# A bank of its own for the mixer's output products, three raw query products begun ahead, and another order in the routed layer's last tiles

## The chip, the cores and the metric

One core of a Trainium2 chip runs the whole network: a cross-attention layer, a state-space mixer and a routed low-rank layer, in float32. The metric is the device time of one execution in microseconds (us). Engines are named as in the profile: PE multiplies matrices (PEld is its weight load), DVE, ACT and POOL work element by element, SP starts the DMA transfers. Each engine takes its instructions in the order in which the program lists them; an instruction waits until the semaphores that it needs are reached, and what stands behind it on that engine waits too.

## The reference, cut to what matters

```python
x = x + xattn(layernorm(x), ctx, mask)   # x: 8 x 64 x 512, ctx: 8 x 1601 x 512
x = x + mixer(layernorm(x))
x = x + routed(layernorm(x))

# xattn: 32 query heads, 8 key heads of 128
q = rmsnorm(hidden @ q_proj_w.T) ; k = rmsnorm(ctx @ k_proj_w.T) ; v = ctx @ v_proj_w.T
out = softmax(q k^T / sqrt(128) + mask) v @ o_proj_w.T

# mixer: 64 heads of 64 channels in 8 groups, 128 states
gate, hbc, dt = split(h @ in_proj_w.T)
xs, B, C = silu(causal_conv4(hbc))
y = scan(state = state * exp(dt * A) + dt * xs * B ; y = state . C) + xs * D
y = y * rsqrt(mean of squares over the group) * norm_weight * silu(gate)
out = y @ out_proj_w.T

# routed: the best of 8 experts by logits = x @ route_w.T, each of rank 16
out = one_hot(argmax) * max(logits) * (x @ A.T) @ Bw
```

## The kernel before, in words

The 512 tokens are four tiles of 128. Nearly all projections are done by a scheme of seven block products in place of eight: a product of 2 x 2 blocks is put together from sums of weight blocks (S1 to S4, made by POOL in `weight_sums`, lines 142 to 150, in the order S1, S2, S3, S4 of which each but S3 needs one before it) and sums of input blocks (T1 to T4, made by DVE). `FIRST` (line 38) lists the products a, d, b, c; a takes raw blocks alone (L11, R11), d takes S2 and T2, b takes S1 and T1, c takes S3 and T3. `SECOND` (line 39) adds three further products into the banks of a, b and c: one of raw blocks, one with S4, one with T4.

**Query stage** (`project_queries`, lines 153 to 305). Sixteen pairs of heads go through `load` (line 172: 512 KB of weights wq_p by SP, then POOL's four sums), `first` (line 215: FIRST on PE, then the ACT copy q_p and the DVE sums q_u, q_t, q_raw), and `second` (line 234), which closes a pair after the next one's `first`. Weight buffers are three deep, and the PSUM banks ab and cd three each, so a pair's load is issued two pairs ahead. `load(0)` and `load(1)` stand in front, then the rest of the constants, 22 warm-up products, the layernorm and transposes of the four tiles (`layernorm_T`, line 124), and T1 to T4 (line 203). After every second pair `factors` (line 243) sums the squares of four heads (qss), makes their inverse root on ACT (qrs), and sends it through memory to be spread over all partitions (qrsb, 1 MB); `finish` (line 259) multiplies (q_st on DVE) and stores the four heads (q_d, 1 MB). The first keys' and values' weights wk and wv (512 KB each, `Loads.weights`, line 894), and the first context tiles (cx) are issued behind the load of pair 10 (`loaded[HQ // 2 - 6]`); their POOL sums stand where that order puts them, and each sum tile is stored at once for later batches.

**Attention** (`attend_all`) then runs over 8 batches x 4 pairs of key heads; the change touches there only where the first two of those stores are issued.

**Mixer** (`mixer_and_routed`, from line 968). For each of the eight groups g, PE makes six input projections (`project`, with the causal convolution on DVE, L1165, and a silu on ACT), while the steps of the group before (mix, scan, gate) stand between them. After the last silu ACT loads the table of exp and ln (line 121), and `decay` makes seg on PE (L1140) and dec on ACT (L1145) for the four tiles of the next group. Then come the gates of the group (`project_gates`, first and second, twice), and among them the four output products of the group before (`project_out`, line 1309: four products mo into one bank, and one DVE instruction, L1316, that adds them to x with the scale rs of `norm`, line 1295, whose sum pss PE makes just before). The order is written by hand with `issue_after`: first(0), mo 0, second(0), mo 1, first(1), mo 2, second(1), mo 3; decay and norm are bound to the table load only, so a planner puts them between. The eight PSUM banks are: pj three deep (projections, gates and mo), seg two (seg, pss and others), px, y0 and y1 one each; px holds the transposes of `layernorm_T` at the mixer's two ends. The last group has no projections behind it, so its own mix and scan stand between its gates (`own`).

**Routed layer** (`route`, line 1334), per tile, after the last group's four mo: layernorm and transposes, ph (PE), the choice of the best expert on DVE (top, rw, first, rw, wh), wt (a transpose on PE), whT (ACT), ro (PE), o = x + ro (DVE), and a store of 256 KB. Each tile's steps stand behind the next tile's mo.

Of the kernel before, what the change touches and what calls it, by code (L numbers as in the profile page):

```python
# [15 lines left out]
P = 128  # L16
# [107 lines left out]
def layernorm_T(nc, c, small, psum, x, tt, dst, tag="tr", bufs=1, pbufs=2, copy=None):  # L124

    st = small.tile([P, 6], F32, tag="ln_st", name="ln_st")
    nc.vector.bn_stats(st, x[:, tt, :])
    mv = small.tile([P, 2], F32, tag="ln_mv", name="ln_mv")
    nc.vector.bn_aggr(mv, st)
    rs = small.tile([P, 1], F32, tag="ln_rs", name="ln_rs")  # L130
    rsqrt_of_mean(nc, rs, mv[:, 1:2], 1.0, c.eps)
    xn = small.tile([P, D], F32, tag="ln_xn", name="ln_xn", bufs=bufs)
    nc.vector.tensor_scalar(
        xn, x[:, tt, :], mv[:, 0:1], rs, op0=ALU.subtract, op1=ALU.mult
    )
    tp = psum.tile([P, DC, P], F32, tag=tag, name="ln_tp", bufs=pbufs)
    for dc in range(DC):
        nc.tensor.transpose(tp[:, dc, :], xn[:, dc * P : (dc + 1) * P], c.ident)
    (copy or nc.vector.tensor_copy)(dst, tp)


def weight_sums(nc, l, out):

    s1, s2, s3, s4 = (out[:, k] for k in range(4))
    add = nc.gpsimd.tensor_tensor
    add(s1, l["L21"], l["L22"], ALU.add)
    add(s2, s1, l["L11"], ALU.subtract)
    add(s3, l["L11"], l["L21"], ALU.subtract)
    add(s4, l["L12"], s2, ALU.subtract)
    return dict(L11=l["L11"], L12=l["L12"], L22=l["L22"], S1=s1, S2=s2, S3=s3, S4=s4)  # L150


@with_exitstack
def project_queries(ctx, tc, c, x, wq, qw, q_d, rs_d):
# [25 lines left out]
        }  # L180
        weights.append(weight_sums(nc, l, wst.tile([P, 4, 2, HD], F32, tag="ws", name=f"wqs_{p}")))

    load(0)
    load(1)
    c.load_rest()
    xnT = big.tile([P, DC, NT], F32, name="xnT")

    warm = ps.tile([P, P], F32, tag="ss", name="warm", bufs=2)
    for _ in range(22):
        nc.tensor.matmul(warm, lhsT=c.ones, rhs=c.ones, start=True, stop=True)  # L190
    for tt in range(NTT):
        layernorm_T(
            nc, c, small, ps, x, tt, xnT[:, :, tt * P : (tt + 1) * P], tag="ss", bufs=2, pbufs=2,
            copy=nc.scalar.copy,
        )
    r = {
        f"R{e + 1}{half + 1}": xnT[:, 2 * e : 2 * e + 2, half * HT : (half + 1) * HT]
# [10 lines left out]
    def product(ps, lhs, rhs, start, stop):  # L208
        for dc in range(2):
            nc.tensor.matmul(  # L210
                ps, lhsT=lhs[:, dc, :], rhs=rhs[:, dc, :], start=start and dc == 0, stop=dc == 1,
                skip_group_check=True,
            )

    def first(p, quad):
        st = Pair()
        st.w, st.q, st.k = weights[p], quad.q, 2 * (p % 2)
        st.ps = {}
        for pair in ("ab", "cd"):
            t = ps.tile([P, 2, HT], F32, tag=pair, name=f"pq_{pair}_{p}", bufs=3)  # L220
            st.ps[pair[0]], st.ps[pair[1]] = t[:, 0, :], t[:, 1, :]

        for k, lhs, rhs in FIRST:
            product(st.ps[k], st.w[lhs], r[rhs], k in "ad", False)
        p1 = wk2.tile([P, HT], F32, tag="p1", name="q_p1")
        nc.scalar.copy(p1, st.ps["a"])
        st.u2 = wk2.tile([P, HT], F32, tag="u2", name="q_u2", bufs=3)
        nc.vector.tensor_tensor(st.u2, p1, st.ps["d"], ALU.add)
        t = wk2.tile([P, HT], F32, tag="t", name="q_t", bufs=1)
        nc.vector.tensor_tensor(t, st.u2, st.ps["b"], ALU.add)  # L230
        nc.vector.tensor_tensor(st.q[:, st.k + 1, HT:], t, st.ps["c"], ALU.add)
        return st
# [41 lines left out]
        )  # L274


    quads, open_ = [], []

    def close():
        st, quad = open_.pop(0)  # L280
# [2 lines left out]
        return quad if len(quad.sq) == 2 else None  # L283

    for p in range(HQ // 2):
        if p % 2 == 0:
            quad = Pair()
            quad.n, quad.sq = p // 2, []
            quad.q = late.tile([P, QD4, NT], F32, tag="q", name="q_raw", bufs=3)
            quads.append(quad)  # L290
        if p + 2 < HQ // 2:
            load(p + 2)
        open_.append((first(p, quad), quad))
        if p:
            done = close()
        if p % 2 == 1 and p > 1:

            factors(quads[p // 2 - 1])
            if p > 3:
                finish(quads[p // 2 - 2])  # L300
# [1 line left out]
    factors(quads[-1])  # L302
    finish(quads[-2])
    finish(quads[-1])
    return loaded[HQ // 2 - 6].ins


@with_exitstack
def attend_all(
# [399 lines left out]
    with tc.issue_after(queries_loaded):  # L709
        first.wk = loads.weights("wk", first)  # L710
        first.wv = loads.weights("wv", first)
        first.cx.load[0]()
        first.cx.load[1]()
        load_mask()
        load_q(first)
    for add in first.cx.sums[0]:
        add()
    def last_projection():
# [99 lines left out]
class Loads:  # L818
# [1 line left out]

    def __init__(self, nc, ctxp, wpool, ctxT, wk, wv, s_d):
        self.nc, self.ctxp, self.wpool, self.ctxT, self.s_d = nc, ctxp, wpool, ctxT, s_d
        self.w = dict(wk=wk, wv=wv)

    def context(self, b):

# [65 lines left out]
    def weights(self, name, u):  # L894

        nc, pr = self.nc, u.pr
        bufs = 1 if name == "wk" else 2
        raw = self.wpool.tile([P, DC, 2 * HD], F32, tag=name, name=f"{name}_{pr}", bufs=bufs)
        nc.sync.dma_start(
            out=raw,  # L900
            in_=self.w[name][:, pr * 2 * HD : (pr + 1) * 2 * HD].rearrange("(dc p) o -> p dc o", p=P),
        )
        l = {
            f"L{hh + 1}{e + 1}": raw[:, 2 * e : 2 * e + 2, hh * HD : (hh + 1) * HD]
            for hh in range(2) for e in range(2)
        }
        sums = self.wpool.tile([P, 4, 2, HD], F32, tag=f"{name}s", name=f"{name}s_{pr}", bufs=bufs)
        s1, s2, s3, s4 = (sums[:, k] for k in range(4))
        if u.b == 0:
            weight_sums(nc, l, sums)  # L910
            nc.sync.dma_start(out=self.s_d[name, pr], in_=sums)
        else:
            nc.sync.dma_start(out=sums, in_=self.s_d[name, pr])
        return dict(raw=raw, L11=l["L11"], L12=l["L12"], L22=l["L22"], S1=s1, S2=s2, S3=s3, S4=s4)
# [3 lines left out]
def cross_attention(ctx, tc, c, x, ctxT, lastT, maskT, wq, wk, wv, wo):  # L918
# [3 lines left out]
    big = ctx.enter_context(tc.tile_pool(name="xa_big", bufs=1))  # L922
    dram = ctx.enter_context(tc.tile_pool(name="xa_dram", bufs=1, space=bass.MemoryType.DRAM))
    qw = big.tile([P, 1], F32, name="qw")

    nc.vector.tensor_scalar(
        qw, c.qnw, c.knw, 1.0 / math.sqrt(HD), op0=ALU.mult, op1=ALU.mult
    )
    mask_sb = big.tile([P, NKT, S], F32, name="mask_sb")

    last_keys = big.tile([P, DC, B], F32, name="last_keys")
# [16 lines left out]
        rows_d.append(r)  # L948

    with tc.tile_pool(name="xa_ctx", bufs=1) as ctxp, tc.tile_pool(name="xa_w", bufs=1) as wpool:  # L950
        loads = Loads(nc, ctxp, wpool, ctxT, wk, wv, s_d)
        queries_loaded = project_queries(tc, c, x, wq, qw, q_d, rs_d)
        full = NKT - 1

        def load_mask():
            nc.sync.dma_start(
                out=mask_sb[:, :full, :], in_=maskT[: full * P, :].rearrange("(t p) q -> p t q", p=P)
            )
            nc.sync.dma_start(out=mask_sb[: KV - full * P, full, :], in_=maskT[full * P :, :])
            nc.sync.dma_start(out=last_keys, in_=lastT.rearrange("(dc p) b -> p dc b", p=P))  # L960

        return attend_all(
            tc, c, x, loads, mask_sb, load_mask, last_keys, q_d, o_d, v1_d, rows_d, wo, queries_loaded
        )
# [3 lines left out]
def mixer_and_routed(ctx, tc, c, x, done, w_in, w_out, w_ra, b_w, out):  # L968
# [337 lines left out]
            G.rs[tt] = rs[:, i : i + 1]  # L1306
        return last.ins

    def project_out(G, tt):
        po = bank("pj", [P, D], "mo", 3)  # L1310
        for n in range(GC):
            last = nc.tensor.matmul(  # L1312
                po, lhsT=G.y[:, n, tt * P : (tt + 1) * P], rhs=G.wo[:, n, :],
                start=n == 0, stop=n == GC - 1,
            )
        nc.vector.scalar_tensor_tensor(  # L1316
            out=x[:, tt, :], in0=po, scalar=G.rs[tt], in1=x[:, tt, :], op0=ALU.mult, op1=ALU.add
        )
        return last.ins
# [10 lines left out]
    def load_routed():  # L1330
        nc.sync.dma_start(out=w, in_=w_ra.rearrange("(dc p) o -> p dc o", p=P))
        nc.sync.dma_start(out=bw, in_=b_w)

    def route(tt):
        xnT = grpp.tile([P, DC, P], F32, tag="sq", name="rt_xnT")
        layernorm_T(nc, c, small, ps, x, tt, xnT, tag="px", bufs=2, pbufs=1, copy=nc.scalar.copy)
        ph = bank("seg", [P, E + E * R], "ph", 2)
        for dc in range(DC):
            nc.tensor.matmul(
# [20 lines left out]
        whT = wk.tile([P, P], F32, tag="whT", name="whT")  # L1360
        nc.scalar.copy(whT, pt)
        po = bank("y1", [P, D], "ro")
        nc.tensor.matmul(po, lhsT=whT, rhs=bw, start=True, stop=True)
        o = wk.tile([P, D], F32, tag="acc", name="o", bufs=3)
        nc.vector.tensor_tensor(o, x[:, tt, :], po, ALU.add)
        nc.sync.dma_start(out=out[tt * P : (tt + 1) * P, :], in_=o)


    g0 = groups[0]
# [97 lines left out]
    with tc.issue_after(table):  # L1467
        norm(G, range(NTT))
        for tt in range(NTT):
            project_out(G, tt)  # L1470
            if tt:
                route(tt - 1)
        route(NTT - 1)


@with_exitstack
# [63 lines left out]
```

## Time and profile before

| what | us |
|---|---|
| time, median of 3 runs | 2778.91 (2778.89 to 2780.34) |
| profiled execution | 2779.38 |
| its span | 2777.7 |
| PE busy in the span | 2739.1 (99%) |
| DVE, POOL, ACT busy | 1748.5, 809.3, 777.4 |
| query stage, first product to first key product | 11.43 to 130.01 |
| attention | 130 to about 2285 |
| mixer and routed layer | about 2285 to 2777.7 |

The mean granted clock of PE is 0.998 of full speed. In the rows that follow, a line of a timeline gives the start, the duration, the engine, the source line, the operation with its output and inputs, and in brackets how long the engine had been idle before and what ended the idle time. A line of the waits gives the waiting instruction, what released it, the total, the number of times and the longest. [...]

### The profile page before, as it was taken

How to read it: one execution, taken by the hardware profiler on the slowest of the kernel's cores; microseconds unless marked ns; L12 is line 12 of the kernel's file. 1: busy time of each engine (PE TensorE's matmuls, PEld its weight loads, DVE VectorE, ACT ScalarE, POOL GpSimd, SP SyncE). 2: the span in 40 equal slices, each digit the busy share in tenths (PEclk: the TensorE clock that was granted, in tenths of full speed). 3: DMA queues.
4: the chain of work that ended last, by engine and by line, in shares of the span. 5: the costliest groups of instructions: out<-in, count | busy, mean ns of one | idle time of the engine just before them, and what ended most of it. 6: DMA issues, size and time to landing. Idle time of an engine off the chain costs nothing.

```text
span 2777.7 us, 39019 instructions
## 1 busy us (share of the span) xinstructions
PE 2739.1 (99%) x14988; PEld 2006.3 (72%) x14988; DVE 1748.5 (63%) x3160; ACT 777.4 (28%) x1410; POOL 809.3 (29%) x818
## 2 busy tenths in 40 slices
PE   9999999999999999999999999999999998999998
PEld 7677777777778777778777777777787544555555
DVE  4556676566666666766666676667666316655666
ACT  3322223222222222223222222322222003333333
POOL 4323323322222233223322222232223113333321
PEclk9999999999999999999999999999999999999999
DMA  4821322231123213221312232122212452333421
GB/s 160 280 87 47 88 68 54 54 104 43 50 54 90 55 39 93 69 56 47 104 47 53 54 89 56 39 82 80 55 41 56 142 194 69 92 106 84 137 58 35
DMA packets 349571, 222.85 MB, mean 80 GB/s; under 512 B 223916, under 2 KB 308778, under 8 KB 348362
## 3 DMA queue, kind: packets, MB, share of 16 engines
q1 hardware_dynamic: 349386, 220.36, 28.2%
q8 instruction: 119, 1.95, 0.3%
q14 instruction: 66, 0.54, 0.1%
HBM read 189.26 MB, written 31.05 MB: 79 GB/s over the span
## 4 chain that ended last, share of the span: by engine, by line
PE 92%; DVE 4%; DMA 2%; issue 1%; ACT 1%; POOL 0%; SPq 0%; DVEq 0%; ACTq 0%; POOLq 0%
PE pav L602 13%; PE psc L532 12%; PE pv_a L451 6%; PE pv_b L451 6%; PE pv_c L451 6%; PE pk_b L391 6%; PE pk_c L391 6%; PE pk_a L391 6%; PE pj L1152 4%; PE mo L1312 4%; PE pv_d L451 3%; PE pk_d L391 3%; PE pj_ab L1210 2%; PE psn L420 2%; PE pq_ab L210 1%; PE pj_cd L1210 1%
## 5 line engine op out<-in xcount | busy, mean ns | idle before, releaser
L537 DVE SCALAR_TENSOR_TENSOR attn<-psc,rk,mask_sb 128x256 f32<-128x256 f32 (+1 forms) x832 | 364.4, 476 | 200.1 <-PE psc L532 192.4
L586 POOL TENSOR_TENSOR sm<-attn 128x512 f32<-128x512 f32 x64 | 81.8, 1279 | 1203.3 <-ACT attn L584 1203.3
L602 PE MATMUL pav<-attn,v 128*128 128x256 f32 (+1 forms) x1664 | 380.3, 379 | 0.0
L532 PE MATMUL psc<-q,kT 128*128 128x256 f32 x1536 | 367.1, 380 | 0.0
L589 POOL TENSOR_TENSOR sm<-sm,attn 128x512 f32<-128x512 f32 x256 | 339.4, 1326 | 29.5 <-DVE attn L580 10.7
L532 PEld LDWEIGHTS psc<-q,kT 128*128 128x128 f32 x1536 | 287.6, 190 | 76.3 <-issue 28.6
L602 PEld LDWEIGHTS pav<-attn,v 128*128 128x128 f32 (+1 forms) x1664 | 311.5, 190 | 42.3 <-issue 1.0
L580 DVE TENSOR_TENSOR attn<-attn,nb 128x1024 f32<-128x1024 f32 x192 | 224.9, 1215 | 49.7 <-ACT nb L577 49.6
L584 ACT ACTIVATE attn<-attn 128x1024 f32<-128x1024 f32 x192 | 203.1, 1058 | 80.7 <-DVE attn L580 77.7
L451 PEld LDWEIGHTS pv_a<-wv,cx 128*128 128x128 f32 x1536 | 193.9, 191 | 28.9 <-issue 22.1
L548 DVE TENSOR_TENSOR mx<-mx,attn 128x512 f32<-128x512 f32 x256 | 210.8, 823 | 2.0
L451 PE MATMUL pv_a<-wv,cx 128*128 128x128 f32 x1536 | 206.8, 277 | 0.0
L391 PE MATMUL pk_a<-cx,wk 128*128 128x417 f32 (+1 forms) x512 | 193.3, 500 | 0.8 <-ACT qrs L115 0.8
L1152 PE MATMUL pj<-mx_xnT,w_in 128*128 128x512 f32 x384 | 177.0, 602 | 0.0
L402 ACT ACTIVATE ksq<-kT 128x834 f32<-128x834 f32 (+1 forms) x128 | 109.3, 872 | 144.6 <-DVE kT L383 144.6
L391 PEld LDWEIGHTS pk_a<-cx,wk 128*128 128x128 f32 x512 | 97.2, 190 | 46.1 <-issue 20.8
L1312 PE MATMUL mo<-w_out,y 128*128 128x512 f32 x256 | 116.9, 597 | 10.5 <-issue 7.8
L1152 PEld LDWEIGHTS pj<-mx_xnT,w_in 128*128 128x128 f32 x384 | 68.8, 190 | 71.0 <-issue 68.7
L577 ACT COPY nb<-nbs 128x256 f32<-128x256 f32 x64 | 24.1, 376 | 301.8 <-DMA nbs<-max_d 285.3
L381 ACT COPY kT<-pk_a 128x384 f32<-128x384 f32 x64 | 31.6, 493 | 267.4 <-PE pk_a L391 267.4
L1165 DVE SCALAR_TENSOR_TENSOR acc<-pj,small_consts,acc 128x504 f32<-128x504 f32 (+1 forms) x144 | 103.9, 724 | 1.1
L649 POOL TENSOR_TENSOR o<-o,f 128x512 f32<-128x512 f32 x31 | 39.4, 1271 | 219.9 <-DMA f<-sums_d 182.2
(244 smaller groups left out, 4423.6 us busy)
## 6 DMA issues: line engine op xcount, KB each, us to landing
wk<-in_wk SPq DMA_DIRECT2D x32, 512.0 KB
wv<-in_wv SPq DMA_DIRECT2D x32, 512.0 KB
w_in<-in_w_in SPq DMA_DIRECT2D x16, 1024.0 KB
wvs<-wv_s_d SPq DMA_DIRECT2D x28, 512.0 KB
wks<-wk_s_d SPq DMA_DIRECT2D x28, 512.0 KB
cx<-in_ctxT SPq DMA_DIRECT2D x16, 834.0 KB
cx<-in_ctxT SPq DMA_DIRECT2D x16, 768.0 KB
wq<-in_wq SPq DMA_DIRECT2D x16, 512.0 KB
```

The source lines that it names most:

```text
L391: nc.tensor.matmul(ps[:, :w], lhsT=u.wk[l][:, dc, :], rhs=u.cx.r[ch][r][:, dc, :], start=start and dc == 0, stop=dc == 1, skip_group_check ...
L402: nc.scalar.activation(sq[ch][:, :, half, :w], u.kT[:, :, half, lo:hi], AF.Square)
L451: nc.tensor.matmul(ps[:, i * HD : (i + 1) * HD], lhsT=u.cx.r[ch][r][:, dc, i * P : (i + 1) * P], rhs=u.wv[l][:, dc, :], start=start and i ...
L532: nc.tensor.matmul(ps[:rows, t - t2, :], lhsT=lhsT, rhs=qh, start=True, stop=True)
L537: nc.vector.scalar_tensor_tensor(out=s.at[:rows, t, :].rearrange("p (h q) -> p h q", h=GQ), in0=ps[:rows, t - t2, :].rearrange("p (h q) -> ...
L548: nc.vector.tensor_tensor(s.mx2, s.mx2, s.at[:, t2 : t2 + 2, :], ALU.max)
L580: nc.vector.tensor_tensor(at[:, k : k + 4, :], at[:, k : k + 4, :], nb.unsqueeze(1).to_broadcast([P, 4, 256]), ALU.add,)
L584: nc.scalar.activation(at[:, k : k + 4, :], at[:, k : k + 4, :], AF.Exp)
L589: nc.gpsimd.tensor_tensor(sm2, sm2, at[:, i : i + 2, :], ALU.add)
L602: nc.tensor.matmul(s.av[:, 0, :], lhsT=u.v[:rows, t, hh, :], rhs=s.at[:rows, t, :], start=t == 0, stop=t == NKT - 1,)
L1152: done = nc.tensor.matmul(pj, lhsT=G.w[:, dc, n, :], rhs=xnT[:, dc, :], start=dc == 0, stop=dc == DC - 1).ins
L1312: last = nc.tensor.matmul(po, lhsT=G.y[:, n, tt * P : (tt + 1) * P], rhs=G.wo[:, n, :], start=n == 0, stop=n == GC - 1,)
```

## The change

- The first product (a) of a pair is split off into `begin`. Pairs 0, 1 and 2 are begun before `first` of pair 0; from pair 3 on a pair is begun just before its `first`. `first` takes b, d, c in place of d, b, c. Three loads stand in front in place of two. The DVE instruction for qw, which stood ahead of the first normalisation, goes behind the last, and the normalisations of tiles 2 and 3 are bound behind those of tiles 0 and 1. 16 warm-up products are left of 22.
- The first wk, wv and context loads are bound to the load of pair 11 in place of pair 10, and POOL's sums for wk and wv (of the first batch) to the last sum of the last query pair. The two stores of those first sums are issued after the first query load of the attention.
- In the program's order of SP the loads of wk and wv now stand behind wq_11 and wq_12, and wq_14 between the two halves of the first context load.
- `project_out` takes the bank px, one deep, in place of pj; the four calls after the last group keep pj.
- In `route`, two small products (`fill`) of ones follow the transposes for tiles 2 and 3 each; the last tile's ro, o and store are made in two halves; and the last tile's steps get the priority that tile 2's had. On PE all of ph of tile 3 then stands before wt and ro of tile 2, and on DVE the steps from top to wh of tile 3 before o of tile 2.

```diff
...
@@ -146,8 +147,8 @@
     add(s1, l["L21"], l["L22"], ALU.add)
     add(s2, s1, l["L11"], ALU.subtract)
     add(s3, l["L11"], l["L21"], ALU.subtract)
-    add(s4, l["L12"], s2, ALU.subtract)
-    return dict(L11=l["L11"], L12=l["L12"], L22=l["L22"], S1=s1, S2=s2, S3=s3, S4=s4)
+    last = add(s4, l["L12"], s2, ALU.subtract).ins
+    return dict(last=last, L11=l["L11"], L12=l["L12"], L22=l["L22"], S1=s1, S2=s2, S3=s3, S4=s4)
 
 
 @with_exitstack
@@ -180,18 +181,29 @@
         }
         weights.append(weight_sums(nc, l, wst.tile([P, 4, 2, HD], F32, tag="ws", name=f"wqs_{p}")))
 
-    load(0)
-    load(1)
-    c.load_rest()
+
+    AHEAD = 3
+    for p in range(AHEAD):
+        load(p)
+        if p == 1:
+            c.load_rest()
     xnT = big.tile([P, DC, NT], F32, name="xnT")
 
     warm = ps.tile([P, P], F32, tag="ss", name="warm", bufs=2)
-    for _ in range(22):
+    for _ in range(16):
         nc.tensor.matmul(warm, lhsT=c.ones, rhs=c.ones, start=True, stop=True)
+    norms = []
     for tt in range(NTT):
-        layernorm_T(
-            nc, c, small, ps, x, tt, xnT[:, :, tt * P : (tt + 1) * P], tag="ss", bufs=2, pbufs=2,
-            copy=nc.scalar.copy,
+
+        with tc.issue_after(norms[tt - 2]) if tt > 1 else nullcontext():
+            norms.append(layernorm_T(
+                nc, c, small, ps, x, tt, xnT[:, :, tt * P : (tt + 1) * P], tag="ss", bufs=2, pbufs=2,
+                copy=nc.scalar.copy,
+            ))
+
+    with tc.issue_after(norms[-1]):
+        nc.vector.tensor_scalar(
+            qw, c.qnw, c.knw, 1.0 / math.sqrt(HD), op0=ALU.mult, op1=ALU.mult
         )
     r = {
         f"R{e + 1}{half + 1}": xnT[:, 2 * e : 2 * e + 2, half * HT : (half + 1) * HT]
@@ -212,16 +224,21 @@
                 skip_group_check=True,
             )
 
-    def first(p, quad):
+    def begin(p, quad):
         st = Pair()
         st.w, st.q, st.k = weights[p], quad.q, 2 * (p % 2)
         st.ps = {}
         for pair in ("ab", "cd"):
             t = ps.tile([P, 2, HT], F32, tag=pair, name=f"pq_{pair}_{p}", bufs=3)
             st.ps[pair[0]], st.ps[pair[1]] = t[:, 0, :], t[:, 1, :]
-
-        for k, lhs, rhs in FIRST:
-            product(st.ps[k], st.w[lhs], r[rhs], k in "ad", False)
+        k, lhs, rhs = FIRST[0]
+        product(st.ps[k], st.w[lhs], r[rhs], True, False)
+        return st
+
+    def first(st):
+
+        for k, lhs, rhs in (FIRST[2], FIRST[1], FIRST[3]):
+            product(st.ps[k], st.w[lhs], r[rhs], k == "d", False)
         p1 = wk2.tile([P, HT], F32, tag="p1", name="q_p1")
         nc.scalar.copy(p1, st.ps["a"])
         st.u2 = wk2.tile([P, HT], F32, tag="u2", name="q_u2", bufs=3)
...
@@ -283,14 +300,18 @@
         return quad if len(quad.sq) == 2 else None
 
     for p in range(HQ // 2):
-        if p % 2 == 0:
-            quad = Pair()
-            quad.n, quad.sq = p // 2, []
-            quad.q = late.tile([P, QD4, NT], F32, tag="q", name="q_raw", bufs=3)
-            quads.append(quad)
-        if p + 2 < HQ // 2:
+        for i in range(AHEAD) if p == 0 else range(p, p + 1) if p >= AHEAD else ():
+            if i % 2 == 0:
+                quad = Pair()
+                quad.n, quad.sq = i // 2, []
+                quad.q = late.tile([P, QD4, NT], F32, tag="q", name="q_raw", bufs=3)
+                quads.append(quad)
+            begun.append((begin(i, quads[i // 2]), quads[i // 2]))
+        if AHEAD <= p + 2 < HQ // 2:
             load(p + 2)
-        open_.append((first(p, quad), quad))
+        st, quad = begun.pop(0)
+        first(st)
+        open_.append((st, quad))
         if p:
             done = close()
         if p % 2 == 1 and p > 1:
@@ -302,7 +323,7 @@
     factors(quads[-1])
     finish(quads[-2])
     finish(quads[-1])
-    return loaded[HQ // 2 - 6].ins
+    return loaded[HQ // 2 - 5].ins, weights[-1]["last"]
 
 
 @with_exitstack
@@ -713,6 +734,7 @@
         first.cx.load[1]()
         load_mask()
         load_q(first)
+        loads.store_sums()
     for add in first.cx.sums[0]:
         add()
     def last_projection():
@@ -820,9 +842,16 @@
 
 
 
-    def __init__(self, nc, ctxp, wpool, ctxT, wk, wv, s_d):
-        self.nc, self.ctxp, self.wpool, self.ctxT, self.s_d = nc, ctxp, wpool, ctxT, s_d
+    def __init__(self, tc, nc, ctxp, wpool, ctxT, wk, wv, s_d):
+        self.tc, self.nc, self.ctxp, self.wpool, self.ctxT, self.s_d = tc, nc, ctxp, wpool, ctxT, s_d
         self.w = dict(wk=wk, wv=wv)
+
+        self.stores = []
+
+    def store_sums(self):
+        for out, sums in self.stores:
+            self.nc.sync.dma_start(out=out, in_=sums)
+        self.stores = None
 
     def context(self, b):
 
@@ -907,8 +936,12 @@
         sums = self.wpool.tile([P, 4, 2, HD], F32, tag=f"{name}s", name=f"{name}s_{pr}", bufs=bufs)
         s1, s2, s3, s4 = (sums[:, k] for k in range(4))
         if u.b == 0:
-            weight_sums(nc, l, sums)
-            nc.sync.dma_start(out=self.s_d[name, pr], in_=sums)
+            with self.tc.issue_after(self.sums_behind):
+                weight_sums(nc, l, sums)
+            if self.stores is None:
+                nc.sync.dma_start(out=self.s_d[name, pr], in_=sums)
+            else:
+                self.stores.append((self.s_d[name, pr], sums))
         else:
             nc.sync.dma_start(out=sums, in_=self.s_d[name, pr])
         return dict(raw=raw, L11=l["L11"], L12=l["L12"], L22=l["L22"], S1=s1, S2=s2, S3=s3, S4=s4)
@@ -922,10 +955,6 @@
     big = ctx.enter_context(tc.tile_pool(name="xa_big", bufs=1))
     dram = ctx.enter_context(tc.tile_pool(name="xa_dram", bufs=1, space=bass.MemoryType.DRAM))
     qw = big.tile([P, 1], F32, name="qw")
-
-    nc.vector.tensor_scalar(
-        qw, c.qnw, c.knw, 1.0 / math.sqrt(HD), op0=ALU.mult, op1=ALU.mult
-    )
     mask_sb = big.tile([P, NKT, S], F32, name="mask_sb")
 
     last_keys = big.tile([P, DC, B], F32, name="last_keys")
...
@@ -1306,8 +1335,8 @@
             G.rs[tt] = rs[:, i : i + 1]
         return last.ins
 
-    def project_out(G, tt):
-        po = bank("pj", [P, D], "mo", 3)
+    def project_out(G, tt, tag="px"):
+        po = bank(tag, [P, D], "mo", 3 if tag == "pj" else 1)
         for n in range(GC):
             last = nc.tensor.matmul(
                 po, lhsT=G.y[:, n, tt * P : (tt + 1) * P], rhs=G.wo[:, n, :],
@@ -1331,9 +1360,17 @@
         nc.sync.dma_start(out=w, in_=w_ra.rearrange("(dc p) o -> p dc o", p=P))
         nc.sync.dma_start(out=bw, in_=b_w)
 
+    def fill(n):
+
+        t = bank("pj", [P, P], "fill", 3)
+        for _ in range(n):
+            nc.tensor.matmul(t, lhsT=c.ones, rhs=c.ones, start=True, stop=True)
+
     def route(tt):
         xnT = grpp.tile([P, DC, P], F32, tag="sq", name="rt_xnT")
         layernorm_T(nc, c, small, ps, x, tt, xnT, tag="px", bufs=2, pbufs=1, copy=nc.scalar.copy)
+        if tt >= NTT - 2:
+            fill(2)
         ph = bank("seg", [P, E + E * R], "ph", 2)
         for dc in range(DC):
             nc.tensor.matmul(
@@ -1360,10 +1397,14 @@
         whT = wk.tile([P, P], F32, tag="whT", name="whT")
         nc.scalar.copy(whT, pt)
         po = bank("y1", [P, D], "ro")
-        nc.tensor.matmul(po, lhsT=whT, rhs=bw, start=True, stop=True)
         o = wk.tile([P, D], F32, tag="acc", name="o", bufs=3)
-        nc.vector.tensor_tensor(o, x[:, tt, :], po, ALU.add)
-        nc.sync.dma_start(out=out[tt * P : (tt + 1) * P, :], in_=o)
+
+        n = 2 if tt == NTT - 1 else 1
+        for k in range(n):
+            cols = slice(k * D // n, (k + 1) * D // n)
+            nc.tensor.matmul(po[:, cols], lhsT=whT, rhs=bw[:, cols], start=True, stop=True)
+            nc.vector.tensor_tensor(o[:, cols], x[:, tt, cols], po[:, cols], ALU.add)
+            nc.sync.dma_start(out=out[tt * P : (tt + 1) * P, cols], in_=o[:, cols])
 
 
     g0 = groups[0]
@@ -1467,10 +1508,13 @@
     with tc.issue_after(table):
         norm(G, range(NTT))
         for tt in range(NTT):
-            project_out(G, tt)
+            project_out(G, tt, "pj")
             if tt:
+                ahead = tc.tile_snap_priority()
                 route(tt - 1)
-        route(NTT - 1)
+
+        with tc.high_priority(offset=tc.tile_snap_priority() - ahead):
+            route(NTT - 1)
 
 
 @with_exitstack
```

More of the change, by code (lines that the diff above doesn't have):

```diff
@@ L132, in layernorm_T @@
     xn = small.tile([P, D], F32, tag="ln_xn", name="ln_xn", bufs=bufs)
-    nc.vector.tensor_scalar(
+    norm = nc.vector.tensor_scalar(
         xn, x[:, tt, :], mv[:, 0:1], rs, op0=ALU.subtract, op1=ALU.mult
@@ L139, in layernorm_T @@
     (copy or nc.vector.tensor_copy)(dst, tp)
+    return norm.ins
 def weight_sums(nc, l, out):
@@ L274, in finish @@
         )
-    quads, open_ = [], []
+    quads, begun, open_ = [], [], []
     def close():
@@ L924, in cross_attention @@
     qw = big.tile([P, 1], F32, name="qw")
-    nc.vector.tensor_scalar(
-        qw, c.qnw, c.knw, 1.0 / math.sqrt(HD), op0=ALU.mult, op1=ALU.mult
-    )
     mask_sb = big.tile([P, NKT, S], F32, name="mask_sb")
@@ L950, in cross_attention @@
     with tc.tile_pool(name="xa_ctx", bufs=1) as ctxp, tc.tile_pool(name="xa_w", bufs=1) as wpool:
-        loads = Loads(nc, ctxp, wpool, ctxT, wk, wv, s_d)
-        queries_loaded = project_queries(tc, c, x, wq, qw, q_d, rs_d)
+        loads = Loads(tc, nc, ctxp, wpool, ctxT, wk, wv, s_d)
+        queries_loaded, loads.sums_behind = project_queries(tc, c, x, wq, qw, q_d, rs_d)
         full = NKT - 1
```

## The prediction

> **What bounds the kernel now.** I read the page first, then the waits of TensorE (PE), the timeline around each wait, the granted clock there, and the chain of the last 37 us.
>
> ```profile
> PE 2739.1 (99%) x14988; PEld 2006.3 (72%) x14988; DVE 1748.5 (63%) x3160; ACT 777.4 (28%) x1410; POOL 809.3 (29%) x818
> ```
>
> PE is busy for 2739.1 of 2777.7 us. No product is removed by the change, so all that it can win is among the 38.6 us without PE work, plus stretches where PE runs at a lower clock. The waits of PE (total us, times, longest) say where the 38.6 lie; these five bear on the change:
>
> ```profile
> PE mo L1312 <- issue: 7.8, 5, 1.7
> PE pq_cd L210 <- POOL wqs L147: 4.7, 3, 2.3
> ...
> PE mo L1312 <- DVE acc L1165: 2.6, 2, 1.8
> ...
> PE wt L1359 <- DVE wh L1352: 1.7, 1, 1.7
> ...
> PE pq_ab L210 <- DMA wq<-in_wq: 0.5, 1, 0.5
> ```
>
> The attention stage (130 to 2285 us) has only some 2.4 us of waits: it is PE throughout, so what the query stage wins is carried through it. The profiled execution took 2779.38 us, 0.47 above the median of 2778.91; I sum on the first and take 0.5 off.
>
> **Query stage.** The timeline at pair 11 of the weights, and the clock (columns: stretch, its length, PE busy, PE clock, DMA share, GB/s):
>
> ```profile
> 83.53 1.03 PE L210 MATMUL pq_ab<-xnT,wq 128*128 128x256 f32 x4
> 86.81 1.74 PE L210 MATMUL pq_cd<-xs,wqs 128*128 128x256 f32 x4 [2.25 <-POOL wqs L147]
> 88.34 1.91 PE L210 MATMUL pq_ab<-xs,wqs 128*128 128x256 f32 x4
> ```
>
> ```profile
> 84.00:88.00 4.00, 1.75 (x7) 0.90 0.83 256
> 88.00:92.00 4.00, 4.00 (x14) 0.67 0.79 268
> ```
>
> A product normally takes 0.86 us from start to start; the two after the wait took 1.5 and 1.7. The clock rows give half clock for 0.10 x 4 / 0.5 = 0.8 us and 0.33 x 4 / 0.5 = 2.6 us, together 3.4.
>
> 1. Pair 11: POOL made eight sums for wk and wv (0.72 us each, 78.95 to 84.7) before this pair's own. The change puts them behind the last query sums: -2.25, and with the wait its half clock goes: four products from 86.81 to 91.19 became 4.4 us instead of about 2.6, -1.75.
> 2. Pair 10 waited 1.38 us (78.25) for sums that began at 75.20, when wq_10 had landed; it was issued at 68.83 with wk and wv (1 MB) right behind it. In the new order wk is issued after wq_11 and wv after wq_12: -1.38. Also b is now taken ahead of d, and needs the first sum only: 0.86 us of cover.
> 3. Pair 14 waited 0.50 (DMA) and 1.11 (POOL). wq_14 took 9.8 us to land behind 768 KB of context, 1 MB of factors and 1 MB of query stores. In the new queue half the context stands behind it, and PE meets it with one and a half products more in hand: -1.61.
> 4. Front: PE now does a of three pairs before it needs sums. It waits for wq_1 and wq_2 (about 10.3 and 12.6), and two transposes queue behind that, so the DVE sums of x start some 0.4 later; at the first d (15.74 before, about 16.15 after) 1.5 products more are done, 1.29 us: -0.9. The shorter warm-up (16 for 22) ends in PE time that waits for the layernorm anyway; so does the moved qw (0.20 us of DVE), whose cover was none: it stood ahead of the first xn.
> 5. New waits. PE would come to pair 14 about 6 us sooner, but everything it needs must too: wq_14 stands behind the factor load of quad 4 in SP's queue, and on DVE four products q_st of quad 4 (waiting for that load) and two context sums of 0.95 us stand ahead of the u and t of pair 14, on which b of its second half waits. DMA moved 12.74 MB from 64 to 112 us, 265 GB/s; without the two sum stores (1 MB, now after the query loads) and in 42 us it would be 278 GB/s, against 350 to 390 in its fullest slices. From 0 to 4.7 us (1.5 queue, 1.7 DVE, 1.5 DMA): half, +2.4.
>
> Sum: -0.9 - 1.38 - 2.25 - 1.75 - 1.61 + 2.4 = -5.5 (from -3.2 to -7.9). The stores of wk and wv sums move later by 20 us or more of slack; nothing.
>
> **Mixer, boundaries of groups 1 to 6.** The timeline of one (all six have the same distances within 0.05 us; group 1 waits only 0.89):
>
> ```profile
> 2489.44 0.71 DVE L1165 SCALAR_TENSOR_TENSOR acc<-pj,small_consts,acc 128x488 f32<-128x488 f32 x1
> ...
> 2490.25 3.67 PE L1312 MATMUL mo<-w_out,y 128*128 128x512 f32 x8 [1.71 <-issue]
> ...
> 2492.76 0.64 ACT L1145 ACTIVATE dec<-seg 128x256 f32<-128x256 f32 x2
> 2493.86 0.66 PE L1140 MATMUL seg<-av,past 64*64 64x256 f32 x8
> ...
> 2498.72 0.95 PE L1299 MATMUL pss<-ones,s 128*128 128x1 f32 x8
> ...
> 2500.24 0.75 DVE L1316 SCALAR_TENSOR_TENSOR x<-mo,rs,x 128x512 f32<-128x512 f32 x1 [0.90 <-ACT rs L1303]
> ```
>
> The first mo waits 1.71 us for a bank of "pj" that the last convolution (ends 2490.15) still reads. With a bank of its own it starts at 2488.54. Two waits come in its place:
>
> - seg of decay 1 needs decay 0's exponentials. They stand on ACT behind the last silu and a table load, both held by that same convolution, so they end at 2493.40 whatever PE does. PE could be there at 2488.54 + 3.61 + 0.43 (half a product now stands ahead of seg) = 2492.58; with 0.10 of signal it starts at 2493.50. Wait 0.92; gain so far 0.36 + 0.43 = 0.79 of the 1.71.
> - The new bank has one buffer. The second mo, next on PE behind pss, must wait until DVE has taken the first out of it (L1316), and that needs rs, made from pss. Before, it began at 2499.53, 1.46 ahead of that instruction's end at 2500.99. After: 2500.99 - 0.79 + 0.10 = 2500.30, where it could have begun at 2498.74: wait 1.56. Queued behind it on PE are the first products of the next gates, which need nothing.
>
> Net +0.77 a boundary, six times: **+4.6**. The third and fourth mo have 2.6 us or more of other products before them, so DVE (idle 7.06 us there) has emptied the bank. In group 1 the first mo gains 0.89 only, but seg then waits hardly: the same end.
>
> Clock. [...] I take 0 and keep up to +10.
>
> ```profile
> 2545.00:2547.00 2.00, 0.29 (x3) 1.00 0.62 98
> ```
>
> **Group 7.** Its boundary waits 0.96. Here three products and four small pg stand between first and second mo, DVE takes the first at about 2722.7, and PE arrives at 2723.2: -1.0 (-0.5 to -1.1).
>
> **Tail.** The chain to the end:
>
> ```profile
> 2768.24 0.11 PE wt L1359
> 2768.35 0.47 PE ph L1339 x4
> 2768.82 1.03 PE ro L1363 x2
> ...
> 2769.87 0.69 DVE o L1365
> 2770.56 0.09 DVE top L1343
> ```
>
> Tile 2's wt, ro and o stand in the middle of tile 3's ph and ahead of its top. In the new order ph(3) runs from 2767.75 to about 2768.75, its steps on DVE take the same 1.20 us to 2769.95; wt(3) waits for ro(2) (ends 2770.3), then 0.34 + 0.3 to 2770.95; ro in halves of 0.52, o in halves of 0.42: last o ends at 2772.5 instead of 2774.34. The four fills lie in the 0.67 us of the copy ahead of ph(2) (0.2 over at most). The last store is 128 KB instead of 256 KB, at most 0.4 of the 3.36 us behind it; taken as 0. **-1.8** (-1.0 to -2.2).
>
> **Sum.** -5.5 + 4.6 - 1.0 - 1.8 = -3.7: 2775.7 in the profiled execution, 2775.2 as a median.
>
> **Rivals.**
> - The boundary pays (chance 0.22). If the second mo finds the bank free, or the schedule on PE gives it other work, 0.79 to 1.7 us are kept in each group: -5 to -8 instead of +4.6, so 2763 to 2768; a milder form, query stage at its full -7.9 and boundaries at +0.5, gives about 2771. For it: DVE is idle there. Against: pss, rs and L1316 follow each other, and pss is right before the second mo.
> - The query stage keeps its waits (0.15). DMA is near its limit there; with the queue, DVE and DMA prices all at their upper end (+4.7), and half clock after one or two boundaries (+3), the time is 2779 to 2782.
> - Slower (0.08): half clock after the second mo's wait in every boundary, 6 x 1.7 = +10, gives 2785 with the query gain as I have it. It decides from about five boundaries on (2775.2 + 5 x 1.7 = 2783.7; the limit is 2784.5). [...]
> - The forecast itself (0.55), with its own range 2772.5 to 2778.
>
> **Numbers.** 0.2%, about what a measurement of this kernel can tell from no change, is 5.6 us: faster ends at 2773.35. Below it lie the first rival and some 0.10 of the forecast's 0.55: 0.32. Slower 0.08, the rest 0.60. The range leaves out the best of the first rival (0.11) and the worst end (0.09): 2770 to 2781.
>
> **What would show it.** In the waits of PE after: mo waiting for the DVE instruction that takes mo out, six times about 1.56, and seg waiting for dec about 0.9 five times; no wait for wqs at pairs 10 and 11; a clock of 1.00 from 84 to 92; attention beginning about 5.5 us sooner; the last o ending about 1.8 us sooner after the last mo. Wrong would be: no wait at the second mo; a clock below 1 near the boundaries; or new waits over 4 us at pairs 12 to 15.

## The result, and the profile after

The changed kernel took 2786.12 us (median of 10 runs, 2781.94 to 2792.32), the one before 2779.28 (10 runs, 2778.88 to 2781.70): ratio 1.0024, interval 1.0015 to 1.0032. It is slower by 0.24%. The forecast was 2775.2 (2770 to 2781). The profiled execution was the longest of the ten, 2792.32 us with a span of 2790.6, 12.9 more than before.

First the page's line of busy times:

```profile
PE 2752.3 (99%) x14986; PEld 2012.3 (72%) x14986; DVE 1752.0 (63%) x3161; ACT 777.4 (28%) x1410; POOL 815.5 (29%) x818
```

PE is busy 13.2 us longer with two instructions fewer (2739.1 us before), and idle for 38.3 us where it was 38.6. As much waiting was added as was removed; the whole loss is PE doing the same work at a lower speed. The waits of PE after:

```profile
PE mo L1341 <- DVE x L1345: 8.3, 6, 1.4
PE seg L1169 <- ACT dec L1174: 6.2, 7, 1.8
...
PE pq_ab L222 <- DMA wq<-in_wq: 3.5, 3, 1.9
PE pk_b L412 <- DVE t L388: 2.4, 4, 0.9
PE pq_cd L222 <- POOL wqs L148: 1.6, 2, 1.1
...
PE ro L1405 <- DVE o L1406: 1.3, 2, 0.8
```

The two waits that the forecast put in place of the old one are there: 1.38 for the bank in all six groups (forecast 1.56), about 0.77 for the exponentials in five (0.92; the other two of the seven are group 0's). Now one boundary on the timeline, and the clock in quarters of a microsecond (stretch, length, PE busy, PE clock, DMA share, GB/s):

```profile
2384.14 0.84 PE L1169 MATMUL seg<-av,past 64*64 64x256 f32 x8
...
2385.45 1.05 PE L1328 MATMUL pss<-ones,s 128*128 128x1 f32 x8 [0.48 <-ACT dec L1174]
...
2387.08 0.75 DVE L1345 SCALAR_TENSOR_TENSOR x<-mo,rs,x 128x512 f32<-128x512 f32 x1 [2.43 <-ACT rs L1332]
...
2387.88 6.51 PE L1341 MATMUL mo<-w_out,y 128*128 128x512 f32 x8 [1.38 <-DVE x L1345]
```

```profile
2386.25:2386.50 0.25, 0.25 (x3) 1.00 0.77 295
2386.50:2386.75 0.25, 0.01 (x1) 0.98 0.29 107
2386.75:2387.00 0.25, 0.00 (x0) 0.50 0.07 25
...
2393.50:2393.75 0.25, 0.25 (x1) 0.86 0.00 0
2393.75:2394.00 0.25, 0.25 (x2) 1.00 0.00 0
```

mo 1 took 6.51 us where an mo takes 3.67: the clock was 0.50 from 2386.7 to 2393.6, two spells of 3.4 us. Note when it fell: at 2386.7 the wait of 1.38 had just begun. In the 3.4 us before that, PE was idle by the profile for only 0.48 + 0.24 = 0.7 us, 21%; with the eight one-column products of pss (1.05) it is 52%.

From the start of the mixer to its last mo, half clock was granted for 30.7 us after the change: 20.5 at four of the six boundaries (two with a spell of 3.4 us, two with two in a row) and 10.2 in group 0. Before it was 3.4, all in group 0. The 27.3 us more at half rate are 13.7 us of work, about what PE is busy longer. The six spells of the changed kernel begin at 2325.30, 2332.13, 2386.74, 2448.18, 2564.24 and 2625.68, whole multiples of 3.413 us apart: in this trace the clock changed only on that beat. Stage by stage in the two profiles: the first key product came at 126.46 instead of 130.01 (-3.55); attention took 1.0 longer; from there to the last mo it was 486.83 instead of 470.40 (+16.43); from the last mo to the end 13.80 instead of 14.73 (-0.93). Sum +12.9.

### The profile page after: what moved, and what is told of

Same layout as the page of the kernel before. It is cut to its first block, busy times and chain, and to the rows that moved or that the text cites. A ratio compares the mean times of both kernels' runs of the same rounds, so it can differ in the third digit from the quotient of the medians.

```text
span 2790.6 us, 39017 instructions
## 1 busy us (share of the span) xinstructions
PE 2752.3 (99%) x14986; PEld 2012.3 (72%) x14986; DVE 1752.0 (63%) x3161; ACT 777.4 (28%) x1410; POOL 815.5 (29%) x818
## 4 chain that ended last, share of the span: by engine, by line
PE 88%; DVE 7%; DMA 3%; ACT 1%; issue 1%; POOL 0%; SPq 0%; DVEq 0%; ACTq 0%; POOLq 0%
PE pav L623 13%; PE psc L553 12%; PE pv_a L472 6%; PE pv_b L472 6%; PE pk_b L412 6%; PE pv_c L472 6%; PE pk_c L412 6%; PE pk_a L412 6%; PE mo L1341 4%; PE pv_d L472 3%; PE pk_d L412 3%; DVE acc L1194 2%; PE pj L1181 2%; PE psn L441 2%; PE pj_ab L1239 2%; PE pvl L495 1%
## 5 line engine op out<-in xcount | busy, mean ns | idle before, releaser
L610 POOL TENSOR_TENSOR sm<-sm,attn 128x512 f32<-128x512 f32 x256 | 339.8, 1327 | 29.5 <-DVE attn L601 10.2
L1341 PE MATMUL mo<-w_out,y 128*128 128x512 f32 x256 | 125.5, 635 | 8.3 <-DVE x L1345 8.3
```

Source lines behind the costliest of these rows:

```text
L610: nc.gpsimd.tensor_tensor(sm2, sm2, at[:, i : i + 2, :], ALU.add)
L1341: last = nc.tensor.matmul(po, lhsT=G.y[:, n, tt * P : (tt + 1) * P], rhs=G.wo[:, n, :], start=n == 0, stop=n == GC - 1,)
```

## The experiments

Each kernel ran in turns with the kernel before on one chip; ratios are to that.

**1 and 2. The bank alone, and everything but the bank.** In e1 the kernel before gets the `project_out` of the change; in e2 the changed kernel gets

```diff
-    def project_out(G, tt, tag="px"):
+    def project_out(G, tt, tag="pj"):
```

> The kernel before with one part of the change: mo 0 to 3 of each group in the one-deep bank px. Theory 1 (the clock): the one-deep bank makes mo 1 wait about 1.4 us for the DVE instruction in six groups, just behind the one-column sums, seg waits about 0.9, and the clock is halved in several windows of 3.4 us behind these waits; waits +4, clock +5 to +8: 2787 to 2791 where the kernel before has 2779.3. Theory 2 (only the waits): +4 from the waits, no more half clock than before: 2783 to 2784.

> The changed kernel with mo back in the three-deep bank pj; query stage and routed layer as changed. Theory 1: no wait of mo 1, half clock as seldom as before: query -3, tail -1: 2775 to 2776. Theory 2: the changed kernel's 2786 less the 4 us of waits: 2781 to 2783, with half clock remaining where it was.

Measured: e1 2788.26 us, 1.0029 (1.0018 to 1.0040); e2 2775.11, 0.9982 (0.9974 to 0.9990). So the bank is the part that costs (8.6 us alone, 11.0 on top of the rest), and the rest of the change is worth 4.6. In e1 the wait of mo for DVE is again 8.3 us in six; the half clock up to the last mo is 13.7 us in its profile, half of it at two boundaries and half in group 0.

**3. The wait kept, PE busy in it.** Between pss and mo 1 PE gets six small products, whose results nobody reads:

```diff
...
+            if old and new and not k:
+                with tc.issue_after(done_out), tc.issue_after(old.summed):
+                    done_out = fill(6)
             if old:
                 with tc.issue_after(done_out):
                     done_out = project_out(old, 2 * k + 1)
```

> The changed kernel with six small products of ones (about 1.35 us, results unused) on PE between the one-column sums and mo 1 of groups 1 to 6: the wait for the bank stays, but PE is busy in it. Theory 1: the time falls by the clock loss of these places, to 2777 to 2780, and nearly all spread between runs goes. Theory 2: nothing changes, 2785 to 2787.

Measured: 2779.37 us (2776.95 to 2781.52), 1.0000 (0.9992 to 1.0008): 6.7 less than the change, though mo 1 starts no sooner after pss (1.38 us after its end, as in the changed kernel). In its profile no half clock is left at the boundaries of groups 1 to 6 (the two spells that remain in the mixer are group 0's). The same boundary as above, and its row of 8 us:

```profile
2382.83 1.05 PE L1328 MATMUL pss<-ones,s 128*128 128x1 f32 x8 [0.48 <-ACT dec L1174]
2383.74 1.58 PE L1344 MATMUL fill<-ones 128*128 128x128 f32 x12
2385.26 3.70 PE L1350 MATMUL mo<-w_out,y 128*128 128x512 f32 x8
```

```profile
2380.00:2388.00 8.00, 7.52 (x47) 1.00 0.44 133
```

The loss behind the waits is the clock.

**4. The waits kept, the sums made wide.** Is it the wait, or what stands beside it? The bank of pss gets 128 columns for each sum, of which the first is read:

```diff
...
-            nc.tensor.matmul(pss[:, i : i + 1], lhsT=G.s1[tt], rhs=c.ones[:, 0:1], start=True, stop=True)
+            nc.tensor.matmul(wide[:, i, :], lhsT=G.s1[tt], rhs=c.ones, start=True, stop=True)
```

> The changed kernel with the four sums pss made 128 columns wide (every column the same sum, one is read) in place of one column: about as long on PE, the waits of mo 1 and seg unchanged. Theory 1a (products of one column count as idle time for the clock, and with them a window passes half idle): nearly all half clock of groups 1 to 6 goes, 2778 to 2781. Theory 1b (the waits alone halve the clock): no change, 2785 to 2788.

Measured: 2780.99 us (2778.84 to 2783.41), 1.0006 (0.9997 to 1.0014), 5.1 less than the change. The same waits of mo as after the change, and in the stretch of the boundary as much PE idle time, but no half clock at any of the six boundaries; first e5's wait, then its timeline and its row of 8 us, then the same of the changed kernel:

```profile
PE mo L1342 <- DVE x L1346: 8.3, 6, 1.4
```

```profile
2383.80 1.16 PE L1329 MATMUL pss<-ones,s 128*128 128x128 f32 x8 [0.48 <-ACT dec L1174]
2386.34 3.70 PE L1342 MATMUL mo<-w_out,y 128*128 128x512 f32 x8 [1.38 <-DVE x L1346]
```

```profile
2380.00:2388.00 8.00, 6.14 (x42) 1.00 0.45 137
```

```profile
2384.00:2392.00 8.00, 6.15 (x22) 0.67 0.33 115
```

6.14 and 6.15 of 8 us busy, and a clock of 1.00 against 0.67. The one-column products (1.05 us by the profile) are what tipped it here, as if they were idle time, or nearly.

The changed kernel's own trace says the same. Cut on the beat of 3.413 us, each boundary has one stretch in which PE was idle most, with pss taken as idle:

| boundary of group | stretch begins | PE idle | idle with pss | clock of the next stretch |
|---|---|---|---|---|
| 1 | 2383.33 | 21% | 52% | 0.50 |
| 2 | 2444.77 | 40% | 71% | 0.50 |
| 3 | 2502.80 | 7% | 38% | 1.00 |
| 4 | 2560.82 | 23% | 53% | 0.50 |
| 5 | 2622.26 | 40% | 71% | 0.50 |
| 6 | 2680.29 | 14% | 45% | 1.00 |

In e1 the two boundaries hit had 69% and 61% with pss, the four spared 48% at most; one of these had PE idle for 40%. PE's idle time by itself does not sort the twelve (21% was hit, 40% was spared); with pss counted as idle it does: the six that were hit have 52% or more, the six that were spared 48% or less. A second spell followed where the first still held idle time of 33% or 18% (groups 1 and 4), and none where it held 0 (groups 2 and 5) or, in e1, 16% and 11%.

**5 and 6. Two ways to have the bank without the wait.** e3 gives px to mo 0 only and leaves mo 1 to 3 in pj; e6 keeps px and puts the first products of the second gates ahead of mo 1 (mo 3 then takes pj, since it follows mo 2 at once):

```diff
-                    done_out = project_out(old, 2 * k)
+                    done_out = project_out(old, 2 * k, "pj" if k else "px")
...
-                    done_out = project_out(old, 2 * k + 1)
+                    done_out = project_out(old, 2 * k + 1, "pj")
```

> The changed kernel with only mo 0 in px, and mo 1 to 3 in pj: mo 0 starts at once, mo 1 has no wait for DVE, the wait of seg for dec (about 0.9) stays. Theory 1: 2771 to 2773 (query -3, tail -1, boundaries -0.8 each). Theory 2: 2786 less 8.3 us of the wait of mo 1: 2777 to 2779.

> The changed kernel with the four products of the second gates (3.4 us) ahead of mo 1 in groups 1 to 6, so that the one-deep bank is empty when mo 1 comes; mo 3 takes a bank pj. Theory 1: no wait of mo 1, the one-column sums stand between full products, no half clock there: 2768 to 2772, as with mo 0 alone in px. Rival (the waits move on to other banks): a new wait of 1 us or more in each group, 2776 or more.

Measured: e3 2769.65 us, 0.9962 (0.9949 to 0.9974), somewhat better than expected; e6 2769.95, 0.9963 (0.9949 to 0.9976). Neither has a wait of mo or half clock at those boundaries. Against e2 (2775.11) e3 gains 5.5 us. Less the wait of 0.96 in group 7, which e2 still has, that is 0.75 a boundary, near the 0.79 worked out for the head start alone, seg's wait included (5.2 us in seven, still there).

**7 and 8. The wait of group 0, which every version has, and the tail.** e7 is e3 with sixteen small products in the 3.9 us wait of group 0 for its convolution. e8 is e7 with a bank each for the two halves of the last ro:

```diff
+            if not g and not k:
+                with tc.issue_after(done), tc.issue_after(new.segged[0]):
+                    done_out = fill(16, "px")
...
+            po = bank("y1", [P, D], "ro") if n == 1 else bank("pj", [P, D // n], f"ro{k}", 3)
```

> The kernel with only mo 0 in px, and 16 small products of ones on PE in the 3.9 us wait of group 0, which every version has. Theory 1: no half clock behind that wait: 1.7 to 3.4 us less than with mo 0 alone in px, 2766 to 2768. Rival (DVE and ACT hold that stretch, the clock costs nothing there): 2769 to 2770.

> As the kernel with mo 0 alone in px and the fill in group 0, and with the two halves of the last ro in two banks of their own in place of one: the tail's two waits of ro for o (0.76 and 0.51) go, 0.8 to 1.2 us less: 2765 to 2767. Rival (the last store sets the end): no change against the one before.

Measured: e7 2765.18 us (2764.45 to 2767.07), 0.9951 (0.9938 to 0.9963), just below the range expected; e8 2766.54 (2763.55 to 2767.36), 0.9952 (0.9939 to 0.9964). The fill is worth 3 to 4.5 us (by the ratios, or by the differences to the kernel before); in e3's profile group 0 has 6.8 us of half clock, in e7's none. The banks can't be told in the time. In the trace the last o ends 9.8 us after the last mo instead of 10.9, and the end of the span is 3.3 instead of 2.8 behind it. First the changed kernel, then e8:

```profile
2784.59 0.69 DVE L1406 TENSOR_TENSOR o<-x,ro 128x512 f32<-128x512 f32 x1 [0.31 <-PE ro L1405]
...
2785.43 0.67 PE L1405 MATMUL ro<-bw,whT 128*128 128x256 f32 x2 [0.76 <-DVE o L1406]
...
2786.61 0.70 PE L1405 MATMUL ro<-bw,whT 128*128 128x256 f32 x2 [0.51 <-DVE o L1406]
```

```profile
2760.23 1.13 PE L1407 MATMUL ro<-bw,whT 128*128 128x256 f32 x4 [0.35 <-ACT whT L1400]
```

**9. The binding of POOL's sums, undone in e8.**

```diff
-            with self.tc.issue_after(self.sums_behind):
-                weight_sums(nc, l, sums)
+            weight_sums(nc, l, sums)
```

> The best version so far (mo 0 alone in px, fill in group 0, last ro in two banks) with POOL's sums for wk and wv no longer bound behind the last query sums; by their loads they fall after the sums of pairs 11 and 12. If that binding is what removed the waits of pairs 10 and 11, waits for wqs of 2 us and more come back at pairs 12 or 13: 2767 to 2770. Rival (the later loads alone did it): no new wait, 2765 to 2767.

Measured: 2764.67 us (2763.68 to 2767.76), 0.9948 (0.9935 to 0.9962), the same as e8: the rival held. The sums of wk came right after those of pair 11 and the sums of wv after pair 12's, and no query pair waited for them. The later loads alone had spread the work; that POOL's sums were bound behind the last pair is worth nothing here. This is the fastest version seen, within what e7 and e8 gave.

**10. The fill of group 0 in the kernel before.** The same sixteen products, nothing else.

> The kernel before with nothing but the 16 small products of ones in the 3.9 us wait of group 0. Theory 1: the one half-clock spell behind that wait (3.4 us in the profile before) goes: 1.5 to 3.5 us less than before, 2776 to 2778. Rival (other engines hold that stretch): no change.

Measured: 2777.22 us (2775.62 to 2781.66), 0.9992 (0.9985 to 0.9998): 2.2 to 2.8 us less, as for one half-clock spell (3.4 us, 1.7 of work) or somewhat more.

## Why the prediction was wrong, point by point

- **Boundaries, waits: right.** Forecast +0.77 each from a wait of 1.56 and one of 0.92; measured six of 1.38, five of 0.77, and in group 1 one of 0.48 ahead of pss. The waits of groups 1 to 6 went from 9.4 us (7.8 + 2.6 less group 7's 0.96) to 12.6: +3.2 against +4.6.
- **Boundaries, clock: this step failed.** "I take 0 and keep up to +10." No run shows that 0 for the new wait: the row that stands by it has a wait among full-width products (1.71 us idle, clock 1.00), and the new wait stands beside one-column ones, so it was not the nearest case. The term that was put at 0 measured 5 to 7 us in the median (e5, e4), and in the profiled run, the longest of the ten, 20.5 us of half clock, 10.2 of work. Group 0 had 6.8 us of half clock more than before in that run, 3.4 of work; it stands ahead of the first mo, so this part is not the bank's. The rival "slower", to which 0.08 was given, is what happened. The +10 that it put on six boundaries is what the profiled run lost, by six spells (3.413 us at 0.50, 1.7 of work each) at four of them. Which boundaries were hit went with the beat, which lay elsewhere in each of two traces (its first stretch begins 0.8 us after the program does here, 2.4 us in e1): in e1's profile it was two of the six.
- **The spread between runs** is the clock too. Over the ten runs the mean granted clock goes from 0.994 in the slowest to 0.998 in one of the two fastest, and 0.001 of 2790 us is 2.8 us. Averaged over the runs it is 0.9964 for the changed kernel and 0.9961 for e1, 0.9977 for the kernel before (27 runs), 0.9983 for e4, 0.9986 for e5 and e2. The spread itself doesn't tell the kernels apart: 10.4 us here, but 6.2 in those 27 runs of the kernel before and 2.7 in the seven of e1.
- **Query stage: right within its range, with two terms that missed.** The waits of pairs 10 and 11 went, as forecast, but for 0.42: from the sums of the fourth quad to those of the sixth 32.42 us became 27.25. The wait at pair 14 did not go (2.02 after, 1.61 before): the new-waits term covered that. The front gained 0.6 to 1.0 in e2, e3 and e4; in the changed kernel's own profile it lost 0.8, since PE was idle for 1.93 and 0.69 us waiting for weights there and the clock fell to 0.50 from 11.1 to 14.5 us. "The shorter warm-up (16 for 22) ends in PE time that waits for the layernorm anyway" left that out:

```profile
9.34 1.10 PE L222 MATMUL pq_ab<-xnT,wq 128*128 128x256 f32 x4 [1.93 <-DMA wq<-in_wq]
11.13 1.22 PE L222 MATMUL pq_ab<-xnT,wq 128*128 128x256 f32 x2 [0.69 <-DMA wq<-in_wq]
```

```profile
8.00:12.00 4.00, 1.97 (x6) 0.88 0.76 277
12.00:16.00 4.00, 3.99 (x17) 0.69 0.02 8
```

  That fewer warm-ups made it likelier was not tried by itself. The cause for pair 11 was named wrongly: the later loads were enough (e9). And the 1.75 us for the half clock behind that pair's wait (three products took the 4.4 us, not four) are not there in every run to be gained: in e10's profile the same wait of 2.26 lies across two stretches of the beat, 32% and 34% idle, and the clock stays at 1.00.
- **"What the query stage wins is carried through it" (through attention): wrong by 1.0 us in the changed kernel's profile and by 2.3 in e2's,** by which attention took longer. The row pk_b <- DVE t grew from 0.4 to 2.4 and 3.1 us: PE came sooner than DVE there, at 845, 1357 and 1870 us. What sets DVE's time at these places was not tried.
- **Group 7: right.** From its first mo to the last of all 45.5 us, 45.6 before, and its wait of 0.96 is gone.
- **Tail: half.** -0.93 for -1.8. ph(3) and the steps to wh(3) moved as forecast, but both halves of ro write the one bank y1: the first half waited 0.76 us for o of tile 2 to be read out, the second 0.51 for the first o. e8 takes these away.

In sum the median came out 10.9 us above the forecast. Of this the clock at the boundaries is 5 to 7; by the profiles, the query stage gained some 2 us less than forecast, attention lost 1 and the tail gained 0.9 less, while the waits at the boundaries were 1.4 cheaper. The 1 to 3 us that remain are not assigned.

## What to carry to other kernels

A bank or buffer that is moved to a pool one deep doesn't remove a wait; it moves it to the next user of that pool, so ask what empties the buffer and what stands just ahead of that (here a sum, two ACT steps and a DVE step, right in front of the next output). A stall of PE is to be priced together with the narrow products beside it and with what the clock does behind it (here 0.50 for 3.4 or 6.8 us), and the clock loss behind a stall that can't be avoided could be bought off here by products whose results nobody reads (e4, 6.7 us less than the change). To put a known risk at nothing needs a row that shows the same case; if there is none, its price belongs in the forecast, not only in the range.

## What the runs showed of the hardware

Four sums of one column (eight products, 1.05 us on PE by the profile) let the granted clock fall to 0.50 where sums of 128 columns (1.16 us) in the same place, with the same waits around them, left it at 1.00. In the trace of the changed kernel the half-clock spells began whole multiples of 3.413 us apart, and each in the mixer lasted one or two of them. Beside full-width products 50% of such a stretch idle left the clock at 1.00 in the kernel before; with one-column products counted as idle, 52% and more tipped it at these boundaries, and 48% and less did not. A wait of 3.9 us in one place, filled with small products whose results are not used, gave 3 to 4.5 us in one kernel and 2 to 3 in another.
